# Layer 0's causal convolution: from four diagonal matmuls to one matmul with the taps on the partitions, in column tiles

## The chip, the cores and the metric

The kernel runs on one core of a Trainium2 chip, in fp32 throughout. The metric is the device time of one launch in microseconds (us). Three runs of the kernel before took 8334.36, 8326.86 and 8333.42 us, median 8333.42 us. The profiled execution is a fourth one: it took 8321.79 us, and its span, from the first to the last instruction, is 8320.0 us.

## The reference, cut to what matters

Two images of 64 x 64 positions and 256 channels go through two layers. Layer 0, the one that is changed, runs a Mamba block over the rows (`mh`) and over the columns (`mv`) of each image, each forwards and backwards, and merges the four results with a linear layer:

```python
xz = x @ in_proj_w.T                        # 256 -> 2 x 512 channels
xi, z = jnp.split(xz, 2, axis=-1)
xc = causal depthwise convolution of xi, 4 taps
xi = silu(xc + conv_b)
dt, Bm, Cm = split(xi @ x_proj_w.T, [16, 32])       # 16 + 16 + 16
dt = softplus(dt @ dt_w.T + dt_b)
dA = exp(dt[..., None] * A)                 # 512 channels x 16 states
dBu = (dt * xi)[..., None] * Bm[:, :, None, :]
h = dA_t * h + dBu_t                        # scan over the 64 positions
y = sum over the 16 states of h * C_t, + xi * D
y = y * silu(z)
return y @ out_w.T
```

Layer 1 is a two-layer Mamba-2 over both axes; its computation is not changed.

## The kernel before, in words

**Tiling.** Channels lie on the 128 partitions. Layer 0 works through 64 blocks (2 images x 2 axes x 16). A block holds four sequences of 64 positions (`SB`, `L`), that is 256 positions (`TB`), for the 512 inner channels, which are four channel tiles (`CT`). The forward and the backward direction stand side by side, so a scan tile has 512 positions (`V`) for each of two channel tiles (`UC`), 128 x 1024 elements. The block's channels are two such halves, u = 0 and 1, and for each half there are 16 states n: 32 turns to a block.

**A turn.** For each (u, n): `decay` (ScalarE, L511) writes exp(dt A); `inflow` makes dt x B; `scan` (VectorE, L845) runs the recurrence; `times_c` multiplies by C (GpSimd, L856, for the states in `POOL_C`, else VectorE, L859); `add` (TensorE, transposing matmuls, L518) sums the states in PSUM in the tile `ps_y`. There are three kinds of `inflow`, by the letter in `B_BY`. G: GpSimd multiplies by a row of B that a DMA has broadcast over the partitions (L826). P: TensorE multiplies a transposed dt x by a diagonal of B (`ps_h<-diag,dtxt`, L514). T: ScalarE scales the transposed dt x (`prepare`, tile `scaled`, of which there is one buffer, L511) and TensorE transposes it back (`ps_h<-ident,scaled`, L518). Before, 16 turns are G, 6 are P and 10 are T.

**A block's head.** `norm_x`, `x_proj` (TensorE), `x_copy` (ScalarE, PSUM to the tile `xi`), then `conv`: for each channel tile and direction four matmuls by diagonal matrices of the taps (`diag_w`, built on GpSimd by `diag_taps`, L591), with the moving positions shifted by j, accumulated in PSUM: `ps_mm<-xi,diag_w`, L514. Two of the four tiles are copied to SBUF by `conv_copy`; `silus` then runs all silus of a block in one go, between two loads of an activation table (L511, L707). `bc_proj` gives dt, B and C; `bc_spread` writes B and C to a DRAM tile `bc_rows` (L723) and at once issues, in the order `ROWS`, every DMA that broadcasts a row back (`b_row`, `c_row`, L732).

**Queues and buffers.** Rows go to pools of three (`b_row`) and four (`c_row`) buffers. A row's DMA is issued from SP's queue, and waits there until the row that held its buffer has been read. SP's queue is in order. `ps_h`, the PSUM tile of a turn, has two buffers, as has `ps_mm`, which the head's matmuls share; `ps_y` has one.

**Order.** Nothing is left to a scheduler. Every step has a time in a table (`STEPS0`, `LEADS` and others; one turn is 1000 units, a block follows the last by 32,000), `plan` and `issue` sort all blocks' steps by these times, and each engine runs its instructions in that order. So neighbouring blocks overlap: the head of one lies within the turns of the one before. The times fix an order; they are no times that the chip keeps. Weights change every 16 blocks (`WEIGHTS0`); the first set's DMAs stand in SP's queue, the later three sets' in ScalarE's.

Of the kernel before, what the change touches and what calls it, by code (L numbers as in the profile page):

```python
# [13 lines left out]
P = 128  # L14
C = 256
# [20 lines left out]
UC = CT // 2  # L36
TURN = 1000
# [4 lines left out]
    (-42908, "norm_x"),  # L42
    (-36767, "x_proj", 0),
    (-36585, "x_copy", 0),
    (-34755, "conv", 1, 0),
    (-34515, "conv", 0, 0),
    (-33645, "conv", 1, 1),
    (-33043, "conv", 0, 1),
    (-32704, "conv_copy", 1),
    (-32342, "conv_copy", 0),  # L50
    (-30551, "x_proj", 1),
    (-28383, "x_copy", 1),
    (-26743, "x_proj", 2),
    (-23322, "x_copy", 2),
    (-20019, "x_proj", 3),
    (-17337, "x_copy", 3),
    (-17250, "conv", 3, 0),
    (-16268, "conv", 2, 0),
    (-15434, "conv", 3, 1),
    (-14415, "conv", 2, 1),  # L60
    (-13222, "silus"),
    (-11201, "bc_proj", 0),
    (-10030, "bc_proj", 1),
    (-9982, "bc_spread"),
    (-7914, "b_back"),
    (-7328, "b_copy"),
    (-7148, "dt_proj", 0, 0),
    (-6695, "dt_proj", 0, 1),
    (-6140, "dt_softplus", 0, 0),
    (-6140, "dt_proj", 1, 0),  # L70
    (-6140, "dt_softplus", 0, 1),
    (-6140, "dt_proj", 1, 1),
    (-6140, "dt_softplus", 1, 0),
    (-6140, "dt_softplus", 1, 1),
    (-2457, "dt_x", 1),
    (-2296, "dt_x", 0),
    (167, "dtx_back", 0, 0),
    (479, "dtx_back", 0, 1),
    (830, "dtx_copy", 0, 0),
    (1637, "dtx_copy", 0, 1),  # L80
    (11154, "dtx_back", 1, 0),
    (11608, "skip", 0),
    (12612, "dtx_copy", 1, 0),
    (12796, "dtx_back", 1, 1),
    (14307, "dtx_copy", 1, 1),
    (16220, "y_copy", 0),
    (22174, "y_back", 0, 0),
    (22385, "y_back", 0, 1),
    (22667, "skip", 1),
    (23616, "gated", 0, 0),  # L90
    (23620, "gated", 0, 1),
    (35135, "y_copy", 1),
    (35668, "y_back", 1, 0),
    (35765, "gated", 1, 0),
    (36300, "y_back", 1, 1),
    (37328, "gated", 1, 1),
    (38904, "out_proj", 0),
    (39887, "out_proj", 1),
    (41624, "out_proj", 2),
    (42423, "out_proj", 3),  # L100
    (43166, "residual"),
# [4 lines left out]
    (-49731, "load_in"),  # L106
    (-48969, "load_cols"),
    (-45832, "diag_taps", 0, 0),
    (-45249, "diag_taps", 0, 1),
    (-44666, "diag_taps", 0, 2),  # L110
    (-44083, "diag_taps", 0, 3),
    (-43500, "diag_taps", 1, 0),
    (-42917, "diag_taps", 1, 1),
    (-42868, "decay_rates"),
    (-42334, "diag_taps", 1, 2),
    (-41751, "diag_taps", 1, 3),
    (-41168, "diag_taps", 2, 0),
    (-40585, "diag_taps", 2, 1),
    (-40002, "diag_taps", 2, 2),
    (-39419, "diag_taps", 2, 3),  # L120
    (-38836, "diag_taps", 3, 0),
    (-38253, "diag_taps", 3, 1),
    (-37670, "diag_taps", 3, 2),
    (-37406, "load_x"),
    (-37087, "diag_taps", 3, 3),
    (-33491, "load_dt"),
    (-7239, "diag_skip", 0),
    (-3574, "diag_skip", 1),
    (90, "diag_skip", 2),
    (3755, "diag_skip", 3),  # L130
    (13271, "load_out"),
# [4 lines left out]
    (-72408, "load", 0),  # L136
    (-70908, "load", 1),
    (-69408, "load", 2),
    (-68408, "stats", 0),
    (-67908, "load", 3),  # L140
    (-67658, "stats", 1),
    (-66908, "stats", 2),
    (-66408, "load", 4),
    (-66158, "stats", 3),
    (-65408, "stats", 4),
    (-64908, "load", 5),
    (-64658, "stats", 5),
    (-63908, "stats", 6),
    (-63408, "load", 6),
    (-63158, "stats", 7),  # L150
    (-62408, "stats", 8),
    (-61908, "load", 7),
    (-61658, "stats", 9),
    (-60908, "stats", 10),
    (-60158, "stats", 11),
    (-59408, "stats", 12),
    (-58658, "stats", 13),
    (-57908, "stats", 14),
    (-57158, "stats", 15),
    (-55908, "moments"),  # L160
    (-55158, "mean_sum"),
    (-54408, "mean_dev"),
    (-53658, "var_sum"),
    (-52908, "factor"),
    (-52158, "offset"),
)
APPLY0 = tuple((-50908 + 1500 * i, "apply", i) for i in range(16))
SPILL0 = tuple((14166 + 2500 * j, "spill", j) for j in range(8))

MERGE_FIRST, MERGE_SECOND = -13218, -6139  # L170
# [5 lines left out]
B_BY = ("GGPPGPTGTGTGTGGT", "TGGGPGGGPGTPTGTT")  # L176
# [4 lines left out]
        (262, None, 226, 641, 2392, 3553),  # L181
        (988, None, -690, 1116, 2152, 2783),
        (1118, -5292, 153, 1524, 1614, 2150),
        (570, -4768, 244, 620, 1942, 3524),
        (2, None, -427, 1189, 2392, 2967),
        (-947, -4106, 14, 1450, 2370, 2683),
        (-235, -1488, 51, 1276, 1424, 2524),
        (-190, None, -1386, 985, 1026, 1585),
        (-1172, -1727, -469, 231, 714, 2278),
        (-919, None, -875, -471, 1437, 1670),  # L190
        (-915, -2333, -644, -36, 14, 1525),
        (-480, None, -1074, -376, 1818, 2665),
        (-1040, -1602, -1381, 535, 1050, 2899),
        (-678, None, -985, 377, 918, 2162),
        (-1385, None, -1210, -397, 640, 1466),
        (-944, -2759, -1379, -345, 91, 589),
    ),
    (
        (-474, -1234, -1097, -13, 220, 2621),
        (-1255, None, -1488, -935, 192, 2012),  # L200
        (-588, None, -2420, -144, 461, 1076),
        (-608, None, -2547, -4, 676, 1467),
        (-2075, None, -1112, -195, 481, 2227),
        (-1316, None, -1610, 6, 1088, 2836),
        (-867, None, -2579, -583, 1577, 3114),
        (-832, None, -2098, 400, 2607, 3262),
        (-1586, None, -634, 189, 3192, 3813),
        (-454, None, -207, 375, 2532, 3326),
        (-2102, -3126, -211, 1806, 2365, 3717),
        (29, None, 289, 2125, 2175, 4103),  # L210
        (724, -63, 1227, 1378, 1978, 3226),
        (430, None, -763, 1222, 3306, 3494),
        (767, 86, 667, 778, 1408, 2651),
        (593, 253, 320, 1556, 2132, 4110),
# [3 lines left out]
POOL_C = ((0, 1, 3, 4, 5, 6, 8, 9, 11, 12, 13), (0, 1, 5, 6, 7, 8, 9, 13, 15))  # L218

ROW_BUFS = 3, 4  # L220

# [83 lines left out]
def seqs(ap):  # L305

    return ap.rearrange("p (s l) -> p s l", l=L)
# [11 lines left out]
def row_order():  # L319

    order = []
    for what, bufs in enumerate(ROW_BUFS):
        turns = [n for n in range(2 * NS0) if what or B_BY[n // NS0][n % NS0] == "G"]
        reads = [TURN * n + LEADS[n // NS0][n % NS0][4 if what else 2] for n in turns]
        for i, n in enumerate(turns):
            time = reads[i - bufs] - (TURN * 2 * NS0 if i < bufs else 0)
            order.append((time, n, what))

    times = [sorted(t for t, _, what in order if what == kind) for kind in range(2)]
    rows = []  # L330
    for kind in range(2):
        turns = sorted(n for _, n, what in order if what == kind)
        rows += [(t, n, kind) for t, n in zip(times[kind], turns)]
    return [(kind, n // NS0, n % NS0) for _, n, kind in sorted(rows)]


ROWS = row_order()


# [16 lines left out]
class Consts:  # L356
    def __init__(self, nc, pool):
# [19 lines left out]
        self.eps_rms = tile_([P, 1], "eps_rms")  # L377
        nc.gpsimd.memset(self.eps_rms, 1e-6)
        self.one = tile_([P, 1], "one")
        nc.gpsimd.memset(self.one, 1.0)  # L380
        self.mean_c = tile_([P, P], "mean_c")
        nc.gpsimd.memset(self.mean_c, 1.0 / C)
        self.mean_di = tile_([P, P], "mean_di")
        nc.gpsimd.memset(self.mean_di, 1.0 / DI)


# [12 lines left out]

        self.eye = tile_([P, L], "eye")  # L400
# [7 lines left out]
class GroupNorm:  # L408
# [3 lines left out]
    def __init__(self, nc, k, pin, pool, bank):  # L412
        self.nc, self.k, self.pin, self.pool, self.bank = nc, k, pin, pool, bank

# [7 lines left out]
    def stats(self, i):  # L422
        if i == 0:
            self.st = self.small([P, KT, NTOK // 512, 6], "gn_stats")
        kt, j, x = self.piece(i)
        self.pin(self.nc.vector.bn_stats(self.st[:, kt, j, :], x))
# [52 lines left out]
def layer0(tc, k, d, big, x, kept):  # L479
# [11 lines left out]
    with ExitStack() as ctx:  # L491
# [24 lines left out]
        def transpose(out, x, start=True, stop=True, order=k.ident):  # L516
            pin(
                nc.tensor.matmul(  # L518
                    out, lhsT=x, rhs=order, start=start, stop=stop, is_transpose=True
                )  # L520
            )

        n_img = x.shape[0]
        fcb = wp.tile([P, KT], F32, name="fcb")
        merged = {m: big_dram(tc, ctx, [P, CT, 2 * C], "w_out_" + m) for m in ("mh", "mv")}

        class Image(GroupNorm):

# [987 lines left out]
```

## Time and profile before

| what | value |
|---|---|
| median of three runs | 8333.42 us |
| profiled execution, its own time / its span | 8321.79 us / 8320.0 us |
| last matmuls of layer 0 on the chain of waits | at 6225.88 us of the span |
| `dbc` written, first and last of 64 blocks | 59.0 and 6091.9 us: 95.8 us a block |
| granted TensorE clock | 0.988 of full speed |
| SP: DMA issues in a block | 2 to `bc_rows`, 16 `b_row`, 32 `c_row` |

The profile page gives each engine's busy time and the costliest groups of instructions, with the mean duration of one and the idle time before them. The view by windows cuts the span into stretches; layer 0 is even from about 100 us to 6000 us, so its numbers are divided by 95.8 us to give a block's share. The view of waits says which engine waited for whom. A busy TensorE is not TensorE at its peak, because matmuls are pipelined: what an instruction takes of TensorE is read from the distance between starts in the timeline.

### The profile page before, as it was taken

To read this page: it belongs to the slowest core of one execution; us is meant where nothing else is said; L and a number is where in the kernel's file an instruction comes from. 1 tells how busy PE (TensorE), PEld (TensorE's weight loads), DVE (VectorE), ACT (ScalarE), POOL (GpSimd) and SP (SyncE) were. 2 spreads that over 40 slices of the span, in tenths; PEclk is the share of its full clock that TensorE was granted. 3 is DMA by queue.
4 is the path that set the end of the run, shared out by engine and by line. 5 is a ranking of instruction groups with operands and counts; after the bars stand their busy time and mean duration, and the time that the engine had idled before them with its cause. 6 is when DMAs were issued, how large, how long until landed. Compare 5 with 4: busy or idle time off the path is not lost. (4 is left out here: it accounts for less than half of the span.)

```text
span 8320.0 us, 158654 instructions
## 1 busy us (share of the span) xinstructions
PE 7999.4 (96%) x59858; PEld 6934.9 (83%) x59858; DVE 7525.5 (90%) x6926; ACT 6713.1 (81%) x11826; POOL 7381.7 (89%) x4164
## 2 busy tenths in 40 slices
PE   8999999999999999999999999999979999999999
PEld 6888888888888878888888888888867888888887
DVE  6999999899999999999999999999988888888887
ACT  5888888788888878888888888888868888888887
POOL 6999999999999999999999999999975776677777
PEclk9999999999999999999999999999999999999999
DMA  4444444444444445444444444444533222222233
GB/s 138 135 138 134 132 136 138 134 135 133 130 134 133 133 149 160 133 132 135 133 138 136 139 134 135 135 136 130 154 113 95 68 76 68 74 72 69 80 102 93
DMA packets 546893, 1014.48 MB, mean 122 GB/s; under 512 B 87760, under 2 KB 104144, under 8 KB 544592
## 3 DMA queue, kind: packets, MB, share of 16 engines
q1 hardware_dynamic: 530624, 982.63, 39.3%
q10 hardware_dynamic: 15504, 21.71, 0.8%
q8 instruction: 474, 7.77, 0.4%
q14 instruction: 291, 2.38, 0.1%
HBM read 978.91 MB, written 25.17 MB: 121 GB/s over the span
## 5 line engine op out<-in xcount | busy, mean ns | idle before, releaser
L856 POOL TENSOR_TENSOR prod<-prod,c_row 128x1024 f32<-128x1024 f32 x1280 | 3007.9, 2372 | 88.7 <-DVE prod L845 82.0
L826 POOL TENSOR_TENSOR b<-dtx,b_row 128x1024 f32<-128x1024 f32 x1024 | 2419.9, 2378 | 162.8 <-DVE prod L845 153.9
L518 PE MATMUL ps_y<-ident,prod 128*128 128x128 f32 x16384 | 2085.0, 276 | 66.3 <-POOL prod L856 53.8
L518 PEld LDWEIGHTS ps_y<-ident,prod 128*128 128x128 f32 x16384 | 1840.6, 142 | 292.8 <-POOL prod L856 144.5
L511 ACT ACTIVATE ps_h<-dt,neg_a 128x512 f32<-128x512 f32 x2048 | 1408.2, 688 | 465.9 <-DVE prod L859 353.7
L845 DVE TENSOR_TENSOR_SCAN prod<-ps_h,b 128x1024 f32<-128x1024 f32 x768 | 1731.4, 2274 | 53.7 <-POOL b L826 30.0
L511 ACT ACTIVATE b<-dt,neg_a 128x512 f32<-128x512 f32 x2048 | 1357.0, 711 | 80.0 <-DVE prod L845 77.3
L511 ACT ACTIVATE scaled<-dtxt,bt 128x256 f32<-128x256 f32 x2560 | 1089.3, 497 | 305.9 <-PE ps_h L518 294.6
L845 DVE TENSOR_TENSOR_SCAN ps_h<-b,ps_h 128x1024 f32<-128x1024 f32 x512 | 1169.9, 2285 | 136.4 <-PE ps_h L514 92.8
L845 DVE TENSOR_TENSOR_SCAN prod<-b,ps_h 128x1024 f32<-128x1024 f32 x512 | 1166.8, 2279 | 61.0 <-PE ps_h L518 35.2
L1026 PE MATMUL ps_mm<-xn,w_in 128*128 128x256 f32 x4608 | 1114.0, 383 | 0.0
L859 DVE TENSOR_TENSOR prod<-ps_h,c_row 128x1024 f32<-128x1024 f32 x768 | 939.9, 1224 | 147.9 <-DVE ps_h L845 85.1
L1026 PEld LDWEIGHTS ps_mm<-xn,w_in 128*128 128x128 f32 x4608 | 849.4, 191 | 100.2
L514 PE MATMUL ps_mm<-xi,diag_w 128*128 128x256 f32 (+3 forms) x4096 | 916.0, 374 | 1.5 <-ACT xi L511 1.5
L514 PE MATMUL ps_h<-diag,dtxt 128*128 128x128 f32 x6144 | 766.4, 278 | 90.6 <-DVE prod L859 61.5
L514 PEld LDWEIGHTS ps_h<-diag,dtxt 128*128 128x128 f32 x6144 | 726.3, 193 | 134.9 <-ACT ps_h L511 74.0
L514 PEld LDWEIGHTS ps_mm<-xi,diag_w 128*128 128x128 f32 x4096 | 751.5, 190 | 79.8 <-issue 1.2
L518 PE MATMUL ps_h<-ident,scaled 128*128 128x128 f32 x5120 | 689.7, 279 | 74.0 <-DVE prod L859 51.3
L518 PEld LDWEIGHTS ps_h<-ident,scaled 128*128 128x128 f32 x5120 | 580.2, 143 | 177.8 <-ACT b L511 71.2
L1113 DVE SCALAR_TENSOR_TENSOR conv<-ps_mm,cols,conv 128x252 f32<-128x252 f32 (+2 forms) x1536 | 631.0, 466 | 5.3 <-ACT conv L1023 5.3
L1381 POOL TENSOR_TENSOR half<-sq 128x512 f32<-128x512 f32 x128 | 163.0, 1273 | 530.8 <-ACT sq L1023 530.8
L845 DVE TENSOR_TENSOR_SCAN ps_h<-ps_h,b 128x1024 f32<-128x1024 f32 x256 | 583.1, 2278 | 0.2 <-ACT ps_h L511 0.2
(144 smaller groups left out, 12272.2 us busy)
## 6 DMA issues: line engine op xcount, KB each, us to landing
c_row<-bc_rows SPq DMA_DIRECT2D x2048, 256.0 KB
b_row<-bc_rows SPq DMA_DIRECT2D x1024, 256.0 KB
spread<-factor_rows SPq DMA_DIRECT2D x512, 256.0 KB
y_in<-y SPq DMA_DIRECT2D x32, 256.0 KB
out_dram<-y_in SPq DMA_DIRECT2D x32, 256.0 KB
XU<-in_x_dram SPq DMA_DIRECT2D x8, 512.0 KB
bc_rows<-dbc SPq DMA_DIRECT2D x128, 32.0 KB
XU<-in_x_dram ACTq DMA_DIRECT2D x8, 512.0 KB
```

Of the source, the lines that this page charges most:

```text
L511: pin(nc.scalar.activation(*args, **kwargs))
L514: pin(nc.tensor.matmul(out, lhsT=lhsT, rhs=rhs, start=start, stop=stop))
L518: nc.tensor.matmul(out, lhsT=x, rhs=order, start=start, stop=stop, is_transpose=True)
L826: pin(nc.gpsimd.tensor_mul(b, self.dtx[u], self.row(u, 0, n)))
L845: nc.vector.tensor_tensor_scan(*(t.rearrange("p c t -> p (c t)") for t in (to, a, b)), 0.0, ALU.mult, ALU.add,)
L856: pin(nc.gpsimd.tensor_mul(prod, prod, self.row(u, 1, n)))
L859: pin(nc.vector.tensor_mul(prod, self.h[u, n], self.row(u, 1, n)))
L1026: pin(nc.tensor.matmul(out, lhsT=lhsT, rhs=rhs, start=start, stop=stop))
L1113: nc.vector.scalar_tensor_tensor(to, seqs(pp)[:, :, : L - j], w[:, TAPS - 1 - j : TAPS - j], to, ALU.mult, ALU.add,)
L1381: pin(nc.gpsimd.tensor_add(half, self.sq2[:, 0:2, :], self.sq2[:, 2:4, :]))
```

## The change

The convolution is done another way. `x_copy` writes the pre-convolution channels of two tiles to one padded tile (`padded`, each sequence of 64 behind three zeros, so `SPAN` = 67 and `WIDE` = 268). A new step `x_shift` copies them by DMA, SBUF to SBUF: for each of four groups of 32 channels and each of four shifts, so that partition 32 j + p of `xs` holds channel p of the group shifted by j. It takes 16 DMAs of 32 x 268 elements for a channel tile, 64 for a block, all in SP's queue, into two buffers (`XI_BUFS`). A matmul then contracts the four taps of 32 channels at once: 128 rows in, 32 columns out, and the four groups write four quarters of PSUM's partitions. The weights are four stacked 32 x 32 diagonals for each direction, tile and group, built by one GpSimd multiplication (`conv_taps`); their taps are loaded by 32 small DMAs (`conv_w`).

```diff
-            def conv(self, c, dr):
-                if dr == 0:
-                    self.pc[c] = ps_mm.tile([P, V], F32, name="ps_mm")
-                ps = self.pc[c][:, dr * TB : (dr + 1) * TB]
-                xi = self.xi[:, c, ::-1] if dr else self.xi[:, c, :]
-                matmul(ps, self.w.diag_w[:, c, TAPS - 1, :], xi, True, False)
-                for j in range(1, TAPS):
-                    matmul(
-                        seqs(ps)[:, :, j:],
-                        self.w.diag_w[:, c, TAPS - 1 - j, :],
-                        seqs(xi)[:, :, : L - j],
-                        False,
-                        j == TAPS - 1,
-                    )
+            def x_shift(self, c):
+                self.xs = getattr(self, "xs", {})
+                self.xs[c] = xp.tile([P, TAPS, WIDE], F32, name="xs")
+                for j in range(TAPS):
+                    for g in range(TAPS):
+                        pin(
+                            nc.sync.dma_start(
+                                out=self.xs[c][j * PARTS : (j + 1) * PARTS, g, :],
+                                in_=self.xi[c // 2][g * PARTS : (g + 1) * PARTS, c % 2, j : j + WIDE],
+                            )
+                        )
+
+            def conv(self, c):
+                self.pc[c] = ps_mm.tile([P, V], F32, name="ps_mm")
+                for dr in range(2):
+                    for g in range(TAPS):
+                        x = self.xs[c][:, g, :].rearrange("p (s x) -> p s x", x=SPAN)
+                        x = x[:, ::-1, : TAPS - 2 : -1] if dr else x[:, :, :L]
+                        matmul(
+                            self.pc[c][g * PARTS : (g + 1) * PARTS, dr * TB : (dr + 1) * TB],
+                            self.w.taps[:, dr, c, g, :],
+                            x,
+                            True,
+                            True,
+                        )
...
-B_BY = ("GGPPGPTGTGTGTGGT", "TGGGPGGGPGTPTGTT")
+B_BY = ("GGPPTPTGTGTGTGGT", "TGGTPGTGPGTPTGTT")
...
-POOL_C = ((0, 1, 3, 4, 5, 6, 8, 9, 11, 12, 13), (0, 1, 5, 6, 7, 8, 9, 13, 15))
+POOL_C = ((0, 1, 3, 4, 6, 8, 9, 11, 12, 13), (0, 1, 4, 5, 6, 7, 9, 10, 13, 15))
...
+XI_BUFS = 2
+PADDED = 1
...
+            def gate_silu(self):
                 act(self.gate, self.gate, AF.Silu)
-                act(self.xc[0], self.xc[0], AF.Silu)
...
-                pin(nc.scalar.preload_act_table_set(LOG_EXP))
+            def x_silu(self, c):
+                u = c // UC
+                if u not in self.xc:
+                    self.xc[u] = three.tile([P, UC, V], F32, name="xc")
+                act(self.xc[u][:, c % UC, :], self.pc[c], AF.Silu, bias=self.w.conv_b[:, c, :])
...
                 for c in (2 * part, 2 * part + 1):
-                    matmul(
-                        self.px[:NX, :], self.w.w_x[:, c, :], self.xc[c // UC][:, c % UC, :], c == 0, c == CT - 1
-                    )
+                    for dr in range(2):
+                        matmul(
+                            self.px[dr * NX : (dr + 1) * NX, :],
+                            self.w.w_x[:, c, :],
+                            self.xc[c // UC][:, c % UC, dr * TB : (dr + 1) * TB],
+                            c == 0,
+                            c == CT - 1,
+                        )
...
+                src = d[self.m + "_cols"].rearrange("(g p) c n -> p c g n", g=TAPS)
+                for dr in range(2):
+                    for j in range(TAPS):
+                        tap = TAPS - 1 - j if dr else j
+                        for c in range(CT):
+                            pin(
+                                self.dma.dma_start(
+                                    out=self.conv_w[j * PARTS : (j + 1) * PARTS, dr, c, :],
+                                    in_=src[:, c, :, tap],
+                                )
+                            )
```

The rest of it: `conv_copy` is gone, and silu reads PSUM with the bias (`x_silu`, one step to a channel tile). `bc_proj` writes the two directions to two halves of the partitions, and `bc_spread` copies them with two instructions. Three turns change from G to T: (0, 4), (1, 3) and (1, 6), so that 13 are G, 6 P and 13 T. The number of products by C on GpSimd stays at 20 of 32, on other states. A row's DMA is now a step of its own with a time (`row_steps`), rather than one of a list issued with `bc_spread`. Every time in `STEPS0`, `WEIGHTS0`, `IMAGE0` and `LEADS` is new, so the order on every engine is. Four constants that layer 1 alone uses are made at its start.

In SP's built order for a block, in steady state, the four `x_shift`s stand like this (c(u, n) and b(u, n) are row DMAs): c(0,0), 16 x `x_shift` 0, b(0,9), c(0,1), 16 x `x_shift` 1, c(0,2), b(0,11), 16 rows, 16 x `x_shift` 3, b(1,5), c(0,15), c(1,0), c(1,1), 16 x `x_shift` 2, c(1,2), c(1,3) and the rest. In ScalarE's, six table loads stand in a block where there were four.

## The prediction

> **What bounds the kernel now.** I read the busy time of the engines by windows first, because a mean over the span mixes layer 0, which changes, with layer 1, which does not. The columns are the busy us of PE, PEld, DVE, ACT and POOL with instruction counts, then the granted clock and the DMA share.
>
> ```profile
> 3000.00:4000.00 1000.00, 966.91 (x6707) 840.07 (x6706) 932.96 (x566) 814.34 (x1397) 966.09 (x467) 0.99 0.45 140
> ```
>
> Over the five windows from 1000 to 6000 us the means are DVE 935, POOL 962 and ACT 814 of 1000. With 95.8 us a block (front table) that is DVE 89.6, POOL 92.2, ACT 78.0 us. POOL and DVE are both near the period, so the next view is who makes DVE wait, here from 1000 to 5000 us, 41.8 blocks (total us, times, longest):
>
> ```profile
> DVE ps_h L845 <- PE ps_h L514: 62.0, 32, 4.3
> DVE prod L859 <- DVE ps_h L845: 55.7, 272, 0.6
> DVE ps_h L845 <- ACT scaled L511: 27.6, 10, 3.1
> DVE prod L859 <- PE ps_y L518: 26.9, 52, 1.7
> DVE prod L845 <- PE ps_h L518: 23.9, 41, 0.6
> DVE prod L845 <- POOL b L826: 22.6, 44, 3.1
> ```
>
> With the smaller lines (9.7 and 5.5 on PE, 13.9 on ACT), a block of DVE waits 3.1 us for PE, 1.0 for ACT, 0.5 for POOL and 1.3 for its own last result. So DVE cannot go below 89.6 + 1.3 = 90.9 us, and 4.6 us is what any relief of the others can give: 64 x 4.6 = 295 us at most.
>
> The costs of what changes come from the groups and the timeline (from 2000 to 5000 us; busy us, mean ns):
>
> ```profile
> L826 POOL TENSOR_TENSOR b<-dtx,b_row 128x1024 f32<-128x1024 f32 x500 | 1183.1, 2382 | 78.9 <-DVE prod L845 73.9 <-DVE ps_h L845 3.3 <-DMA c_row<-bc_rows 1.4
> L511 ACT ACTIVATE scaled<-dtxt,bt 128x256 f32<-128x256 f32 x1256 | 534.5, 497 | 149.6 <-PE ps_h L518 144.4 <-PE ps_mm L518 5.0
> L511 ACT ACT_TABLE_LOAD x62 | 79.5, 1283 | 1.1
> ```
>
> The timeline of PE gives the pace: eight conv instructions from 3005.66 to the next start, 0.211 us each, and eight transposes from 3007.35 to 3008.22, 0.109 each. A matmul of 128x256 is two instructions.
>
> ```profile
> 3005.66 1.85 PE L514 MATMUL ps_mm<-xi,diag_w 128*128 128x256 f32 x8
> 3007.35 1.04 PE L518 MATMUL ps_y<-ident,prod 128*128 128x128 f32 x8
> 3008.22 1.04 PE L518 MATMUL ps_h<-ident,scaled 128*128 128x128 f32 x8
> ```
>
> And SP's queue, which the page does not count as busy. Two issues with nothing between start 0.41 us apart; the rest of the time SP waits for a buffer (2000 to 5000 us):
>
> ```profile
> 4042.95 0.32 SPq L732 DMA_DIRECT2D b_row<-bc_rows  x1
> 4043.36 2.24 SPq L732 DMA_DIRECT2D c_row<-bc_rows  x2
> SPq L732 <- POOL prod L856: 1214.2, 624, 5.6
> ```
>
> **What the Trainium skill says.** "TensorE: Matmul & The Clock Gate", Part 3: matmuls of few columns whose outputs start at partitions 32j run side by side in their column groups, 2.38 times as fast for three. No column tiles of 128 x 32 are in this trace, but layer 1 has tiles of 64 x 64, four of which fit, in fp32:
>
> ```profile
> 7513.06 1.22 PE L1026 MATMUL ps_mm<-mix,xt 64*64 64x64 f32 x64
> ```
>
> 64 instructions in 1.22 us, 0.016 each from start to start, where 64 columns at the pace of the conv (0.211 for 256) would take 0.053 alone: 3.3 times, so it agrees. "DMA: Bandwidth & Descriptors", Anatomy of one DMA: a DMA's semaphore wait happens on the issuing sequencer, before dispatch. SP's 1214 us of waits above are that: what stands behind in the queue waits too. "ScalarE: Activation LUTs", What ACT_TABLE_LOAD costs: 1283 ns plus a drain of about 1380. The trace has 1283, but after the load at 1462.58 us the next activation starts at 1463.88, so I charge 1.28 alone.
>
> **The change, part by part (us a block).**
> PE. Conv was 64 instructions x 0.211 = 13.5. It stays 64, of 256 columns, four abreast: 3.4; saved 10.1. Bounds: 0 saved if they run one by one, 10.1 if they run as in layer 1; I take the latter. `bc_proj`, 8 x 0.43 (the distance of its weight loads in the timeline) = 3.4, becomes 16 x 0.213 two abreast: saved 1.7. Three more T turns: 24 transposes x 0.109 = 2.6 more. Net -9.2.
> POOL. Three b products less, 3 x 2.38 = 7.1; 16 `diag_taps` at 0.62 in 16 blocks become one product of 128x1024, about 2.4: 0.5 less. Net -7.6: 84.6 busy.
> ACT. 12 more `scaled` at 534.5/1256 = 0.426: +5.1; two more table loads +2.6; two `conv_copy` less at 0.65: -1.3; the silu of 128x1024 (1.04) as two of 0.65: +0.3; `dbc` in two halves +0.1. Net +6.8: 84.8.
> DVE: no instruction more or less.
> SP: 45 rows + 2 + 64 = 111 issues x 0.41 = 45.5 instead of 20.5. Bound below: 0.31, the start-to-start of two `factor_rows` issues in layer 1; above: 0.49, that of `spread`. I take 0.41, the `bc_rows` issue being as small. DMA share: 0.45 x 45/48 plus 64 x 34 KB (2.2 MB on 12.3 MB) is about 0.50, so bandwidth stays hidden.
>
> Of PE's 9 us only DVE's waits for it count. I take three quarters of 3.1, and all of POOL's 0.5: -2.8. A rise of ACT's waits by 0.3. For SP, what is queued behind `x_shift` matters: between the release of c(0,0)'s buffer, by the product of (1,12), and the issue of c(0,2) stand 35 issues, 14.4 us, and a row needs about 2.5 more to land (after the two issues above, the windows of 0.5 us show traffic rise at 4044.0 and end by 4046.5). In the same time DVE does six scans at 2.28 and one product at 1.22, 14.9 us, and then wants c(0,2). The row is 2.0 late. I take 0.5 of that as new, because DVE's remaining waits fall into the same stretch. Sum: -2.8 + 0.3 + 0.5 = **-2.0**, times 64 = -128 us.
>
> Once only. The three later weight sets put 32 more issues into ACT's queue: between 0.34 us (a `cols` issue) and 0.64 (a `w_x` issue), 11 to 20 us each time, and instructions behind them wait; I take 10 us each on the end, +30. At the start the 32 issues stand ahead of w_in, about +10, and the first block has its 64 shifts (26 us of SP) in the open, of which I take +15. Together **+55** (30 to 90). Layer 1's four constants fall into its wait of 8.5 us for the spill: 0, and 3 us if that cover went. Moved row DMAs: the row count is 45 for 48, and no row gets a buffer sooner; counted with SP.
>
> Total -128 + 55 = -73 on an execution of 8322, and the median of the runs shown is 12 above that: 8333 - 73 = **8260 us**.
>
> **Rivals.**
> B, SP's queue becomes the path: slower. All of the 2.0 is new, POOL's late release of b(0,9) and c(0,1) holds `x_shift` 1 back by 1, and at the second pair c(0,15) and c(1,3) wait behind 32 issues for 1.5: 4.5 instead of 0.5, so +2.0 a block, 128 + 55 = +183: 8516. It decides at an issue distance of (14.9 - 2.5)/35 = 0.35 us: below, c(0,2) is in time. For it: 0.41 is measured. Against: SP is under half busy, and DVE may be late there for other reasons.
> C, ACT becomes the bound. 84.8 busy, plus its waits for `scaled` (191.2 us in 41.8 blocks = 4.6, times 1.3 = 6.0), for yt (105.0 = 2.5) and dt (83.8 = 2.0) is 95.3, and `x_copy` 1 waits for `x_shift` 1 to read the one padded tile. At 96.6 a block: +0.8 x 64 + 55 = +106: 8440. Against: such waits shrink when PE is faster.
> D, the columns don't run side by side: PE, 967 of 1000 in the five windows, is at 92.6 and with 2.6 at 95.2; at 97 a block, +1.2 x 64 + 55: 8465. Layer 1's tiles speak against it.
>
> **How the numbers follow.** Forecast 0.55, B 0.28, C 0.12, D 0.05. A measurement of this kernel tells 0.2% (17 us) from no change. The forecast's own range is 8130 to 8340, of which the part above 8316 is 0.05 of all. So faster 0.50, same 0.10 (that part, and the lower ends of C and B), slower 0.40. The range 8110 to 8510 leaves out about half of B and the last of the forecast's low end, 0.18.
>
> **What would show it.** Conv groups `ps_mm<-xs,conv_taps` at about 0.05 us from start to start (else D). PE busy falling well below 0.9, POOL by 7 us a block. DVE's waits for PE below 1.2 us a block. In the waits, "DVE prod <- DMA c_row" at under 1 us a block; 3 or more, with SP in unbroken runs of 16 to 33 issues, is B. ACT above 0.93 busy with `scaled` ahead of DVE's waits is C. A period above 95.0 us (50 of fixed cost kept) makes the forecast wrong; a fixed cost under 20 or over 100 makes that term wrong.

## The result: 19% slower

The changed kernel takes 9927.36 us (median of four runs, 9923.14 to 9934.04), the kernel before 8333.89 us in the runs beside it: a ratio of 1.1912, 95% interval 1.1891 to 1.1932. The forecast of 8260 us had the wrong sign, and the time lies far above its range. The profiled execution of the change took 9923.14 us, with a span of 9921.4 us and a granted clock of 0.911.

Where the time went is seen first in the view by windows, the stretch from 3000 to 4000 us of the change (busy us of PE, PEld, DVE, ACT and POOL, then clock, DMA share, GB/s):

```profile
3000.00:4000.00 1000.00, 742.47 (x5412) 632.96 (x5412) 732.58 (x457) 682.19 (x1190) 684.09 (x324) 0.88 0.42 119
```

No engine is busy for more than three quarters of the time, and the DMA engines carry no more than before (0.42 after 0.45). The period of a block, from the first and last `dbc`, is (7692.3 - 98.9)/63 = 120.5 us, where it was 95.8. So 24.8 us came in, and 64 x 24.8 = 1587 of the 1601 us that the spans differ by. The busiest engine, PE, works 0.742 x 120.5 = 89.5 us of a block, so what came in is waits. The view of waits, 2000 to 5000 us, about 25 blocks, names them (us in total, times, longest):

```profile
POOL prod L881 <- DVE prod L870: 609.0, 132, 31.2
DVE prod L884 <- DMA c_row<-bc_rows: 567.3, 71, 14.2
ACT padded L502 <- DMA xs<-padded: 250.3, 25, 11.0
POOL prod L881 <- DMA c_row<-bc_rows: 139.7, 26, 11.4
DVE ps_h L870 <- PE ps_h L509: 39.5, 24, 2.1
```

DVE waits 567.3/25 = 22.7 us a block for `c_row`. Before, it was next to nothing in the same stretch:

```profile
DVE prod L859 <- DMA c_row<-bc_rows: 1.4, 2, 1.1
```

ACT waits 10 us a block to write the one padded tile while it is still being read. The timelines show one block. First SP (start, us, what, how many issues):

```profile
4039.64 10.98 SPq L705 DMA_DIRECT2D xs<-padded  x16
4050.72 0.53 SPq L761 DMA_DIRECT2D b_row<-bc_rows  x1
4051.34 1.32 SPq L761 DMA_DIRECT2D c_row<-bc_rows  x3
4052.76 11.30 SPq L705 DMA_DIRECT2D xs<-padded  x16
4064.16 1.00 SPq L761 DMA_DIRECT2D c_row<-bc_rows  x2
...
4102.77 10.75 SPq L705 DMA_DIRECT2D xs<-padded  x16
4113.62 0.53 SPq L761 DMA_DIRECT2D b_row<-bc_rows  x1
4114.25 0.38 SPq L761 DMA_DIRECT2D c_row<-bc_rows  x1
4114.72 10.01 SPq L705 DMA_DIRECT2D xs<-padded  x16
4124.83 0.53 SPq L761 DMA_DIRECT2D c_row<-bc_rows  x1
```

Sixteen issues of `x_shift` take 10 to 11.3 us, and the rows come out between and behind them. By the built order (one b and three c between the first two bursts, one b and one c between the last two) the first pair is `x_shift` 3 and 2 of a block, and the last pair `x_shift` 0 and 1 of the next, with c(0,2) behind it at 4124.83. Then what DVE and ACT did in that time (in brackets the wait ahead):

```profile
4056.40 1.23 DVE L884 TENSOR_TENSOR prod<-ps_h,c_row 128x1024 f32<-128x1024 f32 x1 [8.93 <-DMA c_row<-bc_rows]
4069.79 1.22 DVE L884 TENSOR_TENSOR prod<-ps_h,c_row 128x1024 f32<-128x1024 f32 x1 [3.87 <-DMA c_row<-bc_rows]
4128.35 1.23 DVE L884 TENSOR_TENSOR prod<-ps_h,c_row 128x1024 f32<-128x1024 f32 x1 [10.97 <-DMA c_row<-bc_rows]
```
```profile
4126.21 0.60 ACT L502 ACTIVATE padded<-ps_mm 128x512 f32<-128x512 f32 x1 [8.00 <-DMA xs<-padded]
```

By the order of DVE's products these rows are c(0,15) and c(1,3), behind `x_shift` 3 and 2, and c(0,2), behind `x_shift` 0 and 1. The waits are 8.93 + 3.87 + 10.97 = 23.8 us, against 24.8 that the period grew by. ACT's wait, from 4118 to 4126 us, lies within DVE's last one. The convolution itself is at its best as cheap as hoped, 16 instructions in 1.07 us on PE's timeline:

```profile
3041.01 1.07 PE L505 MATMUL ps_mm<-xs,conv_taps 128*32 128x256 f32 x16
```

That is so for about a third of those from 2000 to 5000 us; their median is 1.38 us.

**Theories.** 1: SP's in-order queue is the path. 64 issues cost 0.63 us each, in bursts, and whatever waits for SP, rows or windows, waits with them. 2: the bytes or descriptors of the shifts load the DMA engines. 3: the new plan (one padded tile, 13 T turns, six table loads, a new order) is slow by itself.

### The profile page after: what moved, and what is told of

Its sections match the earlier page's. It is cut to its first block, busy times and chain, and to the rows that moved or that the text cites. A ratio compares the mean times of both kernels' runs of the same rounds, so it can differ in the third digit from the quotient of the medians.

```text
span 9921.4 us, 168656 instructions
## 1 busy us (share of the span) xinstructions
PE 7908.4 (80%) x61906; PEld 6769.7 (68%) x61906; DVE 7531.4 (76%) x6931; ACT 7136.7 (72%) x12731; POOL 6927.9 (70%) x3912
## 5 line engine op out<-in xcount | busy, mean ns | idle before, releaser
L851 POOL TENSOR_TENSOR b<-dtx,b_row 128x1024 f32<-128x1024 f32 x832 | 1959.1, 2365 | 285.9 <-DVE ps_h L870 249.1
L502 ACT ACTIVATE ps_h<-dt,neg_a 128x512 f32<-128x512 f32 x1664 | 1146.5, 691 | 846.5 <-DVE prod L884 782.8
L502 ACT ACTIVATE b<-dt,neg_a 128x512 f32<-128x512 f32 x2432 | 1592.3, 710 | 181.4 <-DVE prod L870 170.3
L502 ACT ACTIVATE scaled<-dtxt,bt 128x256 f32<-128x256 f32 x3328 | 1410.1, 495 | 196.4 <-PE ps_h L509 108.8
L870 DVE TENSOR_TENSOR_SCAN prod<-b,ps_h 128x1024 f32<-128x1024 f32 x640 | 1457.2, 2277 | 103.1 <-ACT b L502 60.2
L870 DVE TENSOR_TENSOR_SCAN prod<-ps_h,b 128x1024 f32<-128x1024 f32 x640 | 1441.0, 2275 | 38.6 <-ACT ps_h L502 25.2
L870 DVE TENSOR_TENSOR_SCAN ps_h<-b,ps_h 128x1024 f32<-128x1024 f32 x576 | 1320.4, 2292 | 190.3 <-PE ps_h L509 109.4
L509 PE MATMUL ps_h<-ident,scaled 128*128 128x128 f32 x6656 | 989.8, 286 | 91.7 <-DVE prod L870 63.8
L505 PE MATMUL ps_h<-diag,dtxt 128*128 128x128 f32 x6144 | 886.2, 305 | 209.1 <-DVE prod L884 125.3
L509 PEld LDWEIGHTS ps_h<-ident,scaled 128*128 128x128 f32 x6656 | 793.5, 146 | 246.4 <-ACT scaled L502 139.6
```

Of the source, the lines that this page charges most:

```text
L502: pin(nc.scalar.activation(*args, **kwargs))
L505: pin(nc.tensor.matmul(out, lhsT=lhsT, rhs=rhs, start=start, stop=stop))
L509: nc.tensor.matmul(out, lhsT=x, rhs=order, start=start, stop=stop, is_transpose=True)
L851: pin(nc.gpsimd.tensor_mul(b, self.dtx[u], self.over_tiles(u, 0, n)))
L870: nc.vector.tensor_tensor_scan(*(t.rearrange("p c t -> p (c t)") for t in (to, a, b)), 0.0, ALU.mult, ALU.add,)
```

## The experiments

For each run beyond its time I give the **median period**: the median of the 63 distances between the `dbc` of one block and the next. It leaves out the few long blocks where weights change. It is 94.62 us before and 118.89 in the change. Where a single time is given, it is that of one execution; 23 executions of the kernel before, taken together, lie between 8312 and 8354 us, 0.5% apart.

### Fewer issues, the same bytes

The change issues 16 DMAs of 32 partitions to a channel tile. Two runs move the same bytes in wider DMAs. They leave the gathering out: each partition stays where it is, so the convolution, whose instructions are the same, does not get the rows of a tap as it needs them. The run with 16:

```diff
-                    for g in range(TAPS):
                         pin(nc.sync.dma_start(
-                            out=self.xs[c][j * PARTS : (j + 1) * PARTS, g, :],
-                            in_=self.xi[c // 2][g * PARTS : (g + 1) * PARTS, c % 2, j : j + WIDE],
+                            out=self.xs[c][:, j, :],
+                            in_=self.xi[c // 2][:, c % 2, j : j + WIDE],
                         ))
```

> x_shift issues 4 DMAs a tile, each of all 128 partitions of one window, in place of 16 of 32 partitions: the same bytes and the same number of runs of 1072 B in 16 issues a block, with the partitions left where they are (so the rows of a tap are not gathered as the convolution wants them). Theory 1 (issues on SP): 16 x 0.6 to 0.8 = 10 to 13 us a block, period 94 to 98, about 8250 to 8500. Rival 2 (bytes and descriptors, which are unchanged): 9800 to 10000. Rival 3 (the plan itself): over 9600.

Measured: 8245.58 us, median period 92.20 us, the time a little below my range.

> As the run with 16 issues, but 8 DMAs a tile of 64 partitions: 32 issues a block, the same bytes and runs, partitions left where they are. Theory 1: bursts of 8 issues, 5 us, and 20 us a block; a row is at most half as late: period 102 to 108, 8750 to 9150, between the 16 and the 64. Rival 2 and rival 3: as the change, over 9600. If one issue's time goes with its partitions (64 at twice the time of 32), theory 1 gives no gain here and none with 16.

Measured (two DMAs of 64 partitions for each window): 8803.29 us, median period 101.77 us.

From 64 to 32 issues the period falls by 17.1 us, 0.53 for an issue; from 32 to 16 by 9.6, 0.60 for an issue. The bytes and runs are unchanged, so theory 2 falls. The plan is unchanged, and with 16 issues it is faster than before, so theory 3 falls too. DVE's wait for `c_row` in the run with 16, same stretch:

```profile
DVE prod L883 <- DMA c_row<-bc_rows: 12.7, 21, 2.2
```

### What one issue costs

> Nothing of the reference is computed (zeros go out): 13 groups of 16 DMAs on SP, one group after the other, on an otherwise idle core, to measure from start to start what one issue costs by its shape: 32 partitions x 1072 B from SBUF to SBUF as x_shift has them, the same with 1024 B, 256 B, 16, 64 and 128 partitions, to and from DRAM, the read back of four windows at once, and a row of 2048 B or 1024 B spread over 128 partitions as b_row and c_row are. Theory 1a, the shape sets the cost: x_shift's 0.59 to 0.63 us, a row's 0.35 to 0.41, as in the kernels. Theory 1b, the traffic around sets it (the queue gives back pressure): both 0.3 to 0.41 alone, or x_shift's rises only after the first eight of a group. Whether it goes with the partitions: 128 at four times 32 (2.4 us) or the same.

Measured, SP's timeline (start, us, issues):

```profile
18.51 10.09 SPq L1527 DMA_DIRECT2D ss_dst<-ss_src  x16
...
196.58 10.05 SPq L1527 DMA_DIRECT2D ss_256b_dst<-ss_256b_src  x16
217.13 7.31 SPq L1527 DMA_DIRECT2D sd_side<-sd_src  x16
...
247.90 7.27 SPq L1527 DMA_DIRECT2D ds_dst<-ds_line  x16
...
274.95 7.81 SPq L1527 DMA_DIRECT2D ds32x_dst<-ds32x_line  x16
...
306.26 20.55 SPq L1527 DMA_DIRECT2D row_dst<-row_wide  x16
```

From SBUF to SBUF (`ss`), 0.63 us from start to start, on a core that does nothing else. With 16, 64 and 128 partitions, and with 1024 B, the distances are 0.63 to 0.65; the group of 256 B above has 0.63. To DRAM (`sd`) or from DRAM (`ds`) it is 0.46, and 0.5 on average when one DMA reads four windows. So for these shapes it is the two ends, not the size, that set the price, and no traffic is needed for it. The rows came out otherwise than I expected: the first four distances between rows to 128 partitions (`row`) are 0.39 to 0.70 us, but from the seventh on they are 1.4 to 2.2, so rows issued back to back do slow down; what holds them is not shown.

### The cost without the change

The kernel before gets 64 more issues a block, at the change's times, that nothing waits for. Its rows become steps at their due times, as in the change:

```diff
+    (-35241, "x_extra", 0),
+    (-34641, "x_extra", 1),
+    (-19890, "x_extra", 2),
+    (-17465, "x_extra", 3),
...
+            def x_extra(self, c):
+                for j in range(16):
+                    n = 16 * c + j
+                    pin(nc.sync.dma_start(
+                        out=extra[:PARTS, 2 * n : 2 * n + 2], in_=k.ident[PARTS : 2 * PARTS, :2]))
```

> The kernel before, with its rows as steps of their own at the times that they have in the change, and 64 more DMAs a block on SP at the change's times of x_shift, in four bursts of 16: SBUF to SBUF, 32 partitions x 8 B, into a tile that nobody reads. Nothing waits for them, and they move next to no bytes. Theory 1, the issues alone are the cost (40 us of SP a block): DVE waits over 10 us a block for c_row, median period from 94.6 to 106 to 120, 9050 to 9950. Rival, the loss needs those who wait for the windows (conv, x_copy 1 behind the one padded tile) or the bytes: under 98, under 8550.

Measured: 9364.21 us, median period 112.20, 17.6 us more than before. The tile's group and DVE's largest wait:

```profile
L723 SPq DMA_DIRECT2D extra<-ident x4096: 507/589/1951, 24.5 to 7122.9; - x196
```
```profile
DVE prod L865 <- DMA c_row<-bc_rows: 390.8, 76, 9.3
```

An issue of 8 B a partition lasts 589 ns, as one of 1072 B does in the change (588). Issues alone, with next to no bytes and nobody waiting for their data, cost 17.6 us of median period, where the change cost 24.3; DVE waits 390.8/26.7 = 14.6 us a block for `c_row`. In the change SP also stands at the head of its queue for what the extra DMAs do not need, a free window buffer (63.9 us in the 25 blocks) and `x_copy` (34.6 us), and ACT waits until the windows have been made. How much of the rest of the loss is due to these, and how much to the other plan, is not shown.

> As the run with 64 more DMAs, but four bursts of 4: 16 a block, 10 us of SP. Theory 1 with the threshold that the runs show (10 us a block cost nothing, and above it 0.87 us of period per us of SP): median period 94.2 to 95.5, 8310 to 8390. Without a threshold, 0.87 x 10 = 9 us a block: 103, 8870.

Measured (bursts of 4): 8338.98 us, median period 94.63. Ten microseconds of SP a block, in bursts of 4, are free; there is a threshold. It also shows that rows as steps of their own cost nothing. Whether the threshold lies in the sum of a block or in the length of a burst is not separated: every run near it has both small.

### Rows between the issues

Each of the 64 issues becomes its own step, so that rows go between them:

```diff
+        for c, start, gap in ((0, -35241, 180), (1, -32340, 180), (3, -19890, 270), (2, -17465, 195)):
+            for n in range(TAPS * TAPS):
+                steps.append((start + gap * n, "x_shift", c, n // TAPS, n % TAPS))
```

> The change with its 64 issues as they are, from SBUF to SBUF, but each a step of its own, 180 to 270 thousandths of a turn apart, so that rows go between them in place of behind 16. Theory 1a, rows are late because they stand behind a burst: waits of DVE for c_row under 8 us a block (23 in the change), period 100 to 110, 8600 to 9250, and convolutions later instead. Theory 1b, the stretches are too short for the sum (32 issues of 0.63 and some 8 rows are 24 us where 17 are planned, twice a block), in whatever order: 112 or more, 9400 to 9900.

Measured: 10201.64 us, median period 123.18: theory 1b, with a period over its 112 and a time 300 us above its range. The view of waits, 2000 to 5000 us:

```profile
ACT padded L498 <- DMA xs<-padded: 345.6, 23, 16.7
DVE yg L932 <- PE ps_mm L505: 339.3, 24, 15.7
...
DVE ps_h L865 <- PE ps_h L505: 305.3, 24, 15.6
```

DVE's wait for `c_row` is down to 4.2 us in the whole stretch (POOL's stays, at 154). But now the windows are late: ACT waits for the padded tile 345.6/24.4 = 14 us a block, PE stands behind ACT, and DVE waits (339.3 + 305.3)/24.4 = 26 us for PE. So rows between the issues do not help: the stretch up to the next `x_copy` and to the convolutions is too short for the sum, and the order chooses who pays. Why this order costs 4.3 us a block more than the bursts is not shown.

### By way of DRAM

The windows are made with fewer issues: padded is written to DRAM, and read back with four DMAs a tile, each gathering four groups of channels. The write and the reads stand together in the first run:

```diff
...
+                    self.line[c // 2] = dram.tile([P, 2, WIDE + TAPS - 1], F32, name="line")
+                    pin(nc.sync.dma_start(out=self.line[c // 2], in_=self.xi[c // 2]))
...
+                src = self.line[c // 2][:, c % 2, :].rearrange("(g p) w -> p g w", g=TAPS)
                 for j in range(TAPS):
-                    for g in range(TAPS):
+                    pin(nc.sync.dma_start(out=self.xs[c][j * PARTS : (j + 1) * PARTS, :, :],
+                                          in_=src[:, :, j : j + WIDE]))
```

> The windows are made by way of DRAM: one DMA writes padded out for two channel tiles, and four DMAs a tile (one for each tap, 128 runs of 1072 B each) read the shifted windows back. 18 issues on SP a block in place of 64, more bytes than the change (write and read back), the same plan otherwise. Theory 1, SP's in-order queue is the path (64 issues at 0.63 us are 40 us a block in bursts of 10 us, and rows behind them land late): shifts take 18 x 0.6 to 0.8 = 11 to 14 us, the DVE waits for c_row fall from 23 us a block to under 5, and the period from 120.5 to 94 to 98 us: 8250 to 8500. Rival 2, the bytes or descriptors of the shifts load the DMA engines and delay rows: no better than the change, 9900 or more. Rival 3, the new plan itself (one padded tile, 13 T turns, six table loads) costs the time: over 9600.

Measured: 8695.78 us, 1.0435 times the kernel before (1.0411 to 1.0458), median period 99.79. 18 issues, and still above my range. SP's own waits show why:

```profile
SPq L709 <- DMA line<-padded: 215.0, 59, 6.3
```

SP stands 7 us a block at the read, waiting for the write just ahead of it to land, and the rows stand behind. A wait at the head of the queue costs what an issue does. The next run sets the write apart (`x_out`, right after each `x_copy`) and the reads later:

> As the run by way of DRAM, but with the write as a step of its own right after each x_copy and the reads 1.4 turns or more later (for the second pair behind conv 0 and conv 1), so that SP no longer stands waiting for the write to land (7 us a block there, 18 issues at 0.46 as measured alone, 8.3 us). Theory 1 (whatever holds SP's queue holds the block, a wait at its head as much as an issue): median period from 99.8 to 92 to 94 us, 8150 to 8300. Rival: the bytes through DRAM or the four-window reads (4.7 us to land) delay rows or conv: stays over 8500.

Measured: 8373.13 us, median period 94.73: that wins back two thirds of the 7.6 us between the run just before and the one with 16 issues, but falls short of my range. SP still waited 101.6 us in the stretch for the write of the first pair, and PE 36.9 us for windows. With `conv_w` loaded in 8 DMAs instead of 32:

```diff
-                        for c in range(CT):
-                            pin(self.dma.dma_start(out=self.conv_w[j * PARTS : (j + 1) * PARTS, dr, c, :],
-                                                   in_=src[:, c, :, tap]))
+                        pin(self.dma.dma_start(out=self.conv_w[j * PARTS : (j + 1) * PARTS, dr, :, :],
+                                               in_=src[:, :, :, tap]))
```

> The run before with conv_w loaded in 8 DMAs of 32 x 16 elements in place of 32 of 32 x 4. My fixed cost says that the 32 issues on ACT's queue (some 20 us a weight set) hold the block at the three changes of weights: the long periods there (20 to 49 us above the median in the run with 16 issues, 7 to 13 before the change) fall by 10 to 15 us each, and the start by 10: 30 to 55 us less in all than its neighbour, 8110 to 8250. Rival: the long periods come from the weights' landing or from new order of the plan: no difference above 10 us. It may be the fastest of all: under 8330 in either case.

Measured: 8326.38 us, 0.9989 of before (0.9982 to 0.9996), 47 us less than its neighbour. The median period is the same (94.66). The difference lies in the three blocks where weights change, each 12 to 14 us shorter, and in the first `dbc`, 6 us earlier. My total was again too low. Last, the reads later still, at -30500 and -27000, and the second pair's back at the change's times:

> As the run with few conv_w DMAs, but x_shift 0 and 1 3 and 4.5 turns later (at -30500 and -27000, well before conv 0 at -17841), and x_shift 3 and 2 back at the change's times. In that run SP still stands 3.4 us a block at the first read, waiting for the write to land (104.9 us in 31), and the convolutions of the second pair come 1.0 to 1.4 us late. Theory 1 (18 x 0.47 = 8.5 us of issues and no wait at the queue's head is less than the 10.1 us that cost nothing with 16 issues): median period 94.7 to 92 to 93, 8160 to 8240, faster than before by over 1%. Rival, the trip through DRAM itself (more bytes, 4.7 us to land) keeps the convolutions late: 94 or more, 8280 to 8340.

Measured: **8185.83 us, 0.9825 of before (0.9809 to 0.9841)**, median period 92.14; it beats both kernels. The wait for the write is down to 0.5 us in SP's list, and the stretch shown before and after now reads:

```profile
3000.00:4000.00 1000.00, 924.16 (x7350) 799.34 (x7349) 965.38 (x588) 910.62 (x1611) 927.47 (x441) 0.99 0.58 165
```

DVE is busy 965 of 1000 us; it is the bound, at a DMA share of 0.58, more than the change's 0.42. So bytes were not what the change was short of.

### The price or its absorption

The last question: had the issue cost what I assumed, would the forecast have held? Via DRAM with 16 reads a tile there are 66 issues at 0.46 us:

> By way of DRAM with the write apart, but the read in 16 DMAs of 32 partitions a tile: 66 issues a block at 0.46 us (DRAM at one end) in place of 64 at 0.63 (SBUF at both). It separates the price from its absorption. Theory 1, every us of SP in these stretches is on the path: 64 x 0.17 x 0.85 = 9 us a block less than the change: median period 106 to 111, 9150 to 9450. Rival, only the price was off and the rest of the forecast's working holds: 32 x 0.46 + 3 x 0.41 + 2.5 = 18.5 against 14.9, 3.6 late, a quarter of it new: 0.9 a block, under 8350.

Measured: 9399.81 us, median period 110.42. Price alone was not the fault. It differs by its reads alone from the run with the write apart (median period 94.73), and SP waits 3.2 us a block for the write in both. So 48 more issues at 0.46 us, 22.1 us of SP, cost 15.7 us. SP's timeline around `x_shift` 0 and 1:

```profile
4049.72 0.38 SPq L768 DMA_DIRECT2D c_row<-bc_rows  x1
...
4053.88 7.56 SPq L712 DMA_DIRECT2D xs<-line  x16
4061.53 0.37 SPq L768 DMA_DIRECT2D b_row<-bc_rows  x1
4062.00 0.38 SPq L768 DMA_DIRECT2D c_row<-bc_rows  x1
4062.47 9.32 SPq L712 DMA_DIRECT2D xs<-line  x16
4071.89 1.32 SPq L768 DMA_DIRECT2D c_row<-bc_rows  x3
```

By the built order the row at 4049.72 is c(0,2) and the three from 4071.89 on are c(0,4) to c(0,6): from the one to the others are 22.2 us. The reads come later here than in the change, so it is c(0,5), not c(0,2), that DVE waits for, from 4066.49 us, before the row is even issued:

```profile
4076.78 1.22 DVE L891 TENSOR_TENSOR prod<-ps_h,c_row 128x1024 f32<-128x1024 f32 x1 [10.29 <-DMA c_row<-bc_rows]
```

It is 10.3 late, not the 3.6 that the forecast's working gives for 0.46 us; the wait for the write is part of that. And all of it counts, not a quarter: over the stretch DVE waits 348.9/27.2 = 12.8 us a block for `c_row`, and the period grew by more than that.

Together, with SP's shift time a block (issues by their distance, 0.633 us rounded to 0.63, plus waits for the write; waits for a window buffer or for `x_copy` are left out):

| run | issues x us + wait | SP us | median period |
|---|---|---|---|
| before, 16 more | 16 x 0.63 | 10.1 | 94.63 |
| before, 64 more | 64 x 0.63 | 40.5 | 112.20 |
| via DRAM, reads later | 18 x 0.46 | 8.3 | 92.14 |
| 16 issues | 16 x 0.63 | 10.1 | 92.20 |
| via DRAM, apart | 18 x 0.46 + 3.2 | 11.5 | 94.73 |
| via DRAM, few `conv_w` | 18 x 0.46 + 3.3 | 11.6 | 94.66 |
| via DRAM, together | 18 x 0.46 + 7.2 | 15.5 | 99.79 |
| 32 issues | 32 x 0.63 | 20.3 | 101.77 |
| 66 issues from DRAM | 66 x 0.46 + 3.2 | 33.6 | 110.42 |
| the change | 64 x 0.63 | 40.5 | 118.89 |
| the change, spread | 64 x 0.63 | 40.5 | 123.18 |

About 10 us are free, and the change's 30.4 us above that cost 26.7: 0.88 of each. In the kernel before the same 30.4 us cost 17.6, 0.58 of each, so the share is no constant of the queue. The runs just above the threshold lie higher than a line of 0.88. In the two with 11.5 and 11.6 PE waits for windows as well (36.9 and 28.4 us in the stretch); in the one with 15.5 it does not, and why it lies higher is not shown.

## Why the prediction was wrong, point by point

**The step that failed is SP's term.** The sum took +0.5 us a block for rows behind `x_shift`; DVE's waits for `c_row` came to 22.7. Two parts of the term failed, the price of an issue and the share of the lateness that counts, and the second pair was left out. The other terms held in the main.

**Engines: right in the main.** From the windows 1000 to 6000 us times the period, the change's busy time a block is POOL 84.9 us (predicted 84.6), ACT 84.3 (84.8), DVE 89.4 (89.6). PE in the fastest version is 85.5, where 83.4 was forecast: -7.1 instead of -9.2. The column tiles run at (1.07 - 0.38)/15 = 0.046 us from start to start at their best, with 0.38 the mean duration of one, and nearly always so with 16 issues; rival D falls. ACT is at 0.91 even in the fastest stretch shown; rival C falls. Without SP's share the forecast was -2.5 us a block; the median period fell by 2.4 with 16 issues and 2.5 in the fastest version. The mechanism is there too: in the fastest version DVE waits 1.3 us a block for PE and nearly nothing for POOL, where it was 3.1 and 0.5.

**SP's price: wrong.** "SP: 111 issues x 0.41", bounded by 0.31 and 0.49, took `bc_rows` as the nearest row "being as small". Size is not what counts. The trace before had no DMA from SBUF to SBUF, and this kind costs 0.63, so the upper bound did not hold. With it my own sum for c(0,2) gives 32 x 0.63 + 3 x 0.41 + 2.5 = 23.9 against 14.9: 9.0 late, where the forecast had 2.0. In the block shown c(0,2) is 10.97 late. The 2.5 us was short as well: it was read off traffic that does not end at 4046.5 in its view, and in the change DVE starts 3.5 us after c(0,2) is issued (4124.83 to 4128.35).

**SP's absorption: wrong, and worse.** "I take 0.5 of that as new, because DVE's remaining waits fall into the same stretch" let three quarters go. Those waits are 4.6 us a block in all and cannot hide 9; DVE is the engine nearest its floor, so a late row is late work. And the sum was made for one row behind `x_shift` 0 and 1 only: the second pair, `x_shift` 3 and 2, was left at 0 in the forecast, and costs 8.93 + 3.87 = 12.8 us in the block shown. Even at 0.46 the run with 66 issues is at 9400.

**Rival B: the right mechanism, too small.** It named the late rows, the second pair and `x_shift` 1 held back, with a chance of 0.28, at 4.5 us a block. Measured were 23.8 in the block shown. It carried the same 0.41 into 32 issues twice, and priced the second pair at 1.5 us, an eighth of what it cost; `x_shift` 1 is not held back in the block shown, it starts 0.47 us after c(0,1). Its sign of recognition, unbroken runs of 16 issues and over 3 us a block of waits for `c_row`, is what the trace shows. ACT's wait for the padded tile, listed under rival C, belongs to it too: 10 us a block, at the same time as DVE's.

**Once only: the total about right, the split not.** Predicted +55. The run with 16 issues has it nearly bare: 64 x (92.20 - 94.62) = -155, and its span is 76 shorter, so +79 lies outside the steady blocks. Of this, `conv_w`'s 32 issues are 47 us by the two neighbouring runs, 12 to 14 at each change of weights (predicted 10) and 6 at the start (10). In all some 65 of the 79 us lie in the three periods at the changes of weights, where 30 were predicted, and 15 before the first `dbc`, where 25 were; the two errors partly cancel, which is luck.

## What to carry to other kernels

Count a DMA-issuing queue like an engine: issues times the measured distance for that kind of endpoint, plus every wait at its head, stretch by stretch, against the time until the next row behind it is wanted. If the engine that waits has no slack, count the whole lateness, for every burst. Fewer, wider issues, even by a detour through DRAM with more bytes, turned a loss of 19% into a gain of 1.75%, once no read stood in the queue waiting for the write just ahead of it.

## What the runs showed of the hardware that I had not expected

- An issue from SBUF to SBUF takes 0.63 us of SP from start to start, 0.46 with DRAM at one end. From SBUF to SBUF it is the same for 8 B, 256 B or 1072 B a partition, and for 16 or 128 partitions too.
- Row broadcasts issued back to back on an otherwise idle core slow down within a group of 16: from 0.39 to 0.70 us for the first four distances to 1.4 to 2.2 from the seventh on (16 of 256 KB in 20.55 us).
- The granted clock went with PE's load: 0.99 with PE 967 of 1000 us busy before, 0.88 in the change at 742, 0.99 again at 924. The convolution's 16 instructions take 1.38 us in the median in the change, and 1.08 in the fastest version. I take the lower clock for an effect of the waits and not their cause, since DVE waits 3.3 us a block for PE in the change and 3.1 before; no run tests it.
